# Output projection of all tokens in seven products of quarters, and a new order for the other seven products

## The chip, the cores and the metric

The kernel runs on one core of one Trainium2 chip, as one program in one launch. The metric is the device time of that program in microseconds (us); lower is better. The core has a matrix engine (TensorE, PE in the profile), three engines for elementwise work (VectorE or DVE, ScalarE or ACT, GpSimd or POOL) and a queue that issues the DMA transfers (SyncE or SP). Each engine runs its own instructions in order, and semaphores hold an instruction until what it needs is there. Matrix products go to PSUM, whose banks hold 128 x 512 fp32 values each; GpSimd reads and writes SBUF only in this kernel.

## The reference

All values are fp32. 1024 tokens (2 sequences of 512) of width 512 pass through four layers, each with a layer norm before it and a residual sum after it:

```python
x = x + block_sparse_linear(layernorm(x))
x = x + ffn(layernorm(x))        # gate and up: 512 -> 1792, dequantised; down: 1792 -> 512
x = x + mixer(layernorm(x))
x = x + ffn(layernorm(x))        # the same weights again

def mixer(h):                    # H=128 heads of P=64, INTER=8192, 8 groups, N=128, chunks of 128
    proj = h @ in_proj_w.T       # gate (8192), x (8192), B and C (8 x 128 each), dt (128)
    x, B, C = silu(causal_conv4(proj[x, B, C]))
    dt = softplus(dt + dt_bias);  A_dt = -exp(A_log) * dt
    y  = scan over chunks of (C B^T * decay) x_dt + C state + D * x
    y  = y * rsqrt(mean(y * y) + eps) * norm_w * silu(gate)
    return y @ out_proj_w.T      # 8192 -> 512
```

What the change touches are the matrix products of the mixer's input projection, of the gate and up projections of the feed-forward parts, and the mixer's output projection `y @ out_proj_w.T`.

## The kernel before

**Stages.** `block_sparse`, `ffn` (first), `mixer`, `ffn` (second). The normed input lies transposed in SBUF (`xn_t`: 4 chunks of 128 channels x 1024 tokens). The mixer works through its 8192 inner channels in 32 phases of 256 (two tiles of 128 channels, index j, by two sequences of 512 tokens, index b: four "units"). Phase `ph` runs three things side by side: the input projection of its own channels (x first, the gate later), the scan of the channels of the phase before (`c1`), and the output projection of the channels of the phase before that (`ph - 2`). Phases 2 to 30 are called `mid`; there are 29 of them. In seven of them (3, 7, ... 27) a new group of B and C channels is projected as well.

**Order.** Inside the kernel PE, ACT and DVE run in the order in which the program text issues their instructions (`manual_schedule`). The order of GpSimd and of the DMA queue is found by the framework's planner. So the places of `next(steps)`, `next(gate)`, `o()`, `drain(n)`, `flush()`, `back_scores(k)`, `all_squares()` in the phase loop are a schedule written by hand.

**Seven products of quarters.** A product of two matrices, each cut into 2 x 2 quarters, takes eight products of quarters; with sums of quarters made beforehand (Strassen's scheme in Winograd's form) seven do. `seven` (L177) does so for the projections: `left_sides` (L166, GpSimd) makes four sums of the weight's quarters, `tq` holds sums of the input's quarters, each of the seven products is two fp32 matmuls of 128 x 128 by 128 x 512 (each of which shows as two instructions in the profile), and the results are combined by accumulation in PSUM banks x, y, z, by one ScalarE copy (L202) and by five VectorE additions (L206, L211, L212, L220, L225). `seven` is a generator: each `next` issues one product with its sums, and the caller puts other work between. `done(j, b, result)` is called as a result is ready: for x, B and C that is `conv` (L730), one ScalarE pass and three VectorE taps that are kept back until `drain`; for the gate it notes a `silu` for later; in the feed-forward part it is the silu or the multiplication with it.

**Output projection.** In a `mid` phase the token blocks 0, 1, 4 and 5 (the first half of each sequence) go through `out_seven` (L1007): seven products of quarters, each two token blocks by 256 of the 512 columns, whose sums over phases are kept in `acc` (which is `x_sb`) and, for the product that three quarters share, in `common`. `o()` issues one of them with its VectorE sum (L1035). `out_left` (L998) makes four sums of the scan's outputs, `out_right` (L985) four of the weights, all on GpSimd. The blocks 2, 3, 6 and 7 go through `out_project` (L952) by `outs(k)`: two matmuls of 512 columns for each block and one VectorE addition (L969). The first phase and the last ones project all blocks by `out_project`; `merge` (L1055) adds `common` to the three quarters in phase 31.

**The other steps of a phase.** `tokens(k)` transposes one unit (PE, L828), multiplies it with dt (DVE, L832) and with the decay (GpSimd `x_dec`, L836). `back_scores(k)` and `half_scores(k)` make the decay matrix of one head (ACT, L893, L900, L903; GpSimd, L907); its product with the scores (DVE, L901) is kept back until `flush`. `both_states` multiplies `x_dec` with B (PE, L849) and carries states (DVE, L860, L863). `scan` (L915) issues the products of a unit into bank `py` (L920, L929); `skipped` (L940) reads that bank and `gated` (L943) gates the result; `all_squares` squares it (ACT, L949) and sums the squares (GpSimd, L950).

**PSUM.** Eight banks: three of tag `proj`, three of `yo` and two of `tr`. A bank is taken again when its last reader is done. The `yo` banks serve in one phase for the products of the output projection, for the two scans of `half_scan(units[:2])`, for the plain blocks and, in a phase without a new group, for two banks of the gate's seven. The weight tiles `w` of the input projection have two buffers; a DMA fills one (L606) as soon as the last product that reads its former content is done, and `left_sides` (L171 to L174) follows.

## Time and profile before

| What | Value |
|---|---|
| Runs | 2259.35, 2258.80, 2258.38 us; median 2258.8 |
| Span of the profiled execution, first to last instruction | 2256.4 us |
| TensorE granted clock, mean | 1.000 |
| HBM read and written | 194.91 MB and 4.72 MB |
| Busy in 400 to 1026 us (626.0) | PE 623.71, DVE 543.49, ACT 398.19, POOL 368.03 |
| Busy in 1182 to 1900 us (718.0) | PE 718.00, DVE 625.06, ACT 453.90, POOL 417.04 |
| Additions of `seven`, each | 0.68 to 0.69 us on DVE |
| Copy of `seven` (L202), each | 0.57 to 0.59 us on ACT |

The profile is of one execution. It gives its span; the runs' times hold also what lies before the first and behind the last instruction. "Busy" of TensorE comes from pipelined instructions: an instruction of 512 columns is shown as some 0.59 us long, though the next one starts 0.43 us after it. Durations are therefore best read from stretches of like instructions. In lists of groups the columns are line, engine and operation, output and inputs with their sizes and the number of instructions, then busy time in all, mean ns of one, and idle time before them with what ended it. In a timeline the columns are start, length, and the instruction or a run of like ones; in square brackets stands idle time before it and what ended it.

### The profile page before, as it was taken

Reading aid. Unit: us, or ns where it says so; the run is one execution under the profiler, and the core shown is the slowest. Engines: PE = TensorE matmul, PEld = TensorE weight load, DVE = VectorE, ACT = ScalarE, POOL = GpSimd, SP = SyncE. Lnnn points to the kernel's source line nnn. Section 1 sums busy time; section 2 is a strip of 40 time slices with the busy share of each in tenths; the row PEclk is TensorE's granted clock in tenths of the full one; section 3 lists DMA queues with packets and bytes.
Section 4 is the critical chain, followed back from the end, with each engine's and each line's share of the span. In section 5 each row is a group of like instructions: output and inputs, shape, how many; then the busy total and the mean of one; then the engine's idle time right before and its main releaser. Section 6 shows DMA issues by size and latency. Waiting matters only on the chain.

```text
span 2256.4 us, 29331 instructions
## 1 busy us (share of the span) xinstructions
PE 2241.1 (99%) x10356; PEld 1340.5 (59%) x10356; DVE 1766.8 (78%) x3017; ACT 1166.2 (52%) x2474; POOL 1193.9 (53%) x1202
## 2 busy tenths in 40 slices
PE   9999999999999999999999999999999999999999
PEld 5445875556665665665566656656655666544468
DVE  5456558888888888888888888888888989865552
ACT  4111056756665665666566656656665665731100
POOL 3765023655655566566556555665665564536610
PEclk9999999999999999999999999999999999999999
DMA  6563021222222222222222222221222322337500
GB/s 196 191 202 108 24 70 61 80 66 76 74 69 73 76 75 85 65 77 82 66 77 70 71 75 74 77 84 60 82 76 67 111 66 75 122 103 232 196 10 28
DMA packets 145779, 201.53 MB, mean 89 GB/s; under 512 B 7136, under 2 KB 92000, under 8 KB 145632
## 3 DMA queue, kind: packets, MB, share of 16 engines
q1 hardware_dynamic: 145056, 198.61, 27.7%
q8 instruction: 82, 1.34, 0.2%
q10 hardware_dynamic: 576, 1.05, 0.1%
q14 instruction: 65, 0.53, 0.1%
HBM read 194.91 MB, written 4.72 MB: 88 GB/s over the span
## 4 chain that ended last, share of the span: by engine, by line
PE 95%; DVE 3%; ACT 1%; issue 0%; POOL 0%; DVEq 0%; ACTq 0%; POOLq 0%
PE proj L185 31%; PE yo L185 19%; PE po L957 11%; PE po L1022 8%; PE ffn_o L557 7%; PE py L920 5%; PE pst L849 4%; PE py L929 4%; PE x_tr L828 2%; PE pg L487 1%; PE bs_o L336 1%; PE pu L487 1%; PE pgm L779 1%; DVE xc L735 1%; PE ln_tr L142 0%; PE stir L233 0%
## 5 line engine op out<-in xcount | busy, mean ns | idle before, releaser
L907 POOL TENSOR_TENSOR ce<-ce,c_t 128x384 f32<-128x384 f32 x256 | 288.5, 1131 | 318.3 <-ACT ce L903 312.6
L185 PE MATMUL proj<-xn_t,w 128*128 128x512 f32 x824 | 384.6, 593 | 2.0 <-DVE gt L206 1.7
L893 ACT ACTIVATE m<-bc,acs 128x128 f32<-128x128 f32 x1024 | 324.8, 389 | 6.8 <-PE py L920 5.8
L185 PEld LDWEIGHTS proj<-xn_t,w 128*128 128x128 f32 x824 | 153.0, 190 | 155.8 <-issue 146.3
L957 PE MATMUL po<-wo,gt 128*128 128x512 f32 x528 | 238.2, 599 | 0.4 <-DVE y L940 0.4
L171 POOL TENSOR_TENSOR ws<-w 128x256 f32<-128x256 f32 x96 | 74.0, 771 | 308.7 <-DMA w<-in_win_t_dram 269.9
L901 DVE TENSOR_TENSOR m<-m,gm 128x512 f32<-128x512 f32 x256 | 227.6, 907 | 11.3 <-ACT m L900 10.4
L735 DVE SCALAR_TENSOR_TENSOR xc<-proj,cw,xc 128x511 f32<-128x511 f32 (+2 forms) x288 | 214.6, 746 | 6.6
L950 POOL TENSOR_TENSOR sq_acc<-sq_acc,y 128x512 f32<-128x512 f32 x128 | 175.8, 1377 | 76.7 <-ACT y L949 76.5
L185 PE MATMUL proj<-tq,ws 128*128 128x512 f32 x432 | 199.2, 592 | 0.0
L920 PE MATMUL py<-m,x_dt 128*64 128x128 f32 x2048 | 181.4, 276 | 0.1
L900 ACT ACTIVATE m<-m 128x512 f32<-128x512 f32 x256 | 161.3, 630 | 7.4
L957 PEld LDWEIGHTS po<-wo,gt 128*128 128x128 f32 x528 | 96.3, 190 | 109.7 <-issue 103.9
L185 PE MATMUL yo<-tq,ws 128*128 128x512 f32 x336 | 153.4, 599 | 0.4 <-ACT acs L715 0.4
L185 PE MATMUL yo<-xn_t,w 128*128 128x512 f32 x328 | 151.0, 592 | 0.0
L929 PE MATMUL py<-ce,state 128*64 128x128 f32 x1536 | 149.7, 273 | 0.0
L920 PEld LDWEIGHTS py<-m,x_dt 128*64 128x64 f32 x2048 | 122.5, 137 | 30.0 <-issue 14.4
L949 ACT ACTIVATE y<-y 128x512 f32<-128x512 f32 x128 | 76.5, 623 | 110.3 <-DVE gt L943 110.3
L969 DVE TENSOR_TENSOR x_sb<-x_sb,po 128x512 f32<-128x512 f32 x136 | 92.9, 685 | 48.9 <-PE po L957 47.2
L903 ACT ACTIVATE ce<-bc 128x384 f32<-128x384 f32 x256 | 129.8, 507 | 0.0
L245 POOL TENSOR_TENSOR w<-w,sf 128x1024 f32<-128x1024 f32 (+1 forms) x30 | 70.0, 2335 | 112.9 <-DVE w L244 87.2
L732 ACT ACTIVATE xc<-proj,cb,cw 128x512 f32<-128x512 f32 x96 | 74.2, 775 | 105.8 <-DVE proj L225 76.6
(229 smaller groups left out, 4491.7 us busy)
## 6 DMA issues: line engine op xcount, KB each, us to landing
bc<-acs_d SPq DMA_DIRECT2D x128, 512.0 KB, 3.8
w<-in_win_t_dram SPq DMA_DIRECT2D x64, 512.0 KB, 3.8
wo<-in_wo_t_dram SPq DMA_DIRECT2D x31, 512.0 KB, 4.0
wi<-in_down_w_dram SPq DMA_DIRECT2D x14, 512.0 KB, 3.9
zi<-in_down_z_dram SPq DMA_DIRECT2D x14, 512.0 KB, 4.7
sf<-in_down_s_dram SPq DMA_DIRECT2D x14, 512.0 KB, 4.3
wi<-in_gate_w_dram SPq DMA_DIRECT2D x13, 512.0 KB, 4.2
zi<-in_gate_z_dram SPq DMA_DIRECT2D x13, 512.0 KB, 5.3
```

Source lines behind the costliest of these rows:

```text
L185: nc.tensor.matmul(ps, lhsT=a[:, kc, :], rhs=b[:, kc, :], start=(start and kc == 0), stop=(stop and kc == KH - 1), skip_group_check=True,)
L557: nc.tensor.matmul(ps, lhsT=a[:, k, :], rhs=b(k), start=(start and k == 0), stop=(stop and k == KF - 1), skip_group_check=True,)
L735: nc.vector.scalar_tensor_tensor(dst[:, s:], ps[:, : SEQ - s], cw[:, t, 3 - s : 4 - s], dst[:, s:], ALU.mult, ALU.add)
L893: nc.scalar.activation(m[:, c, :], bc[:, hh, c * P : (c + 1) * P], AF.Relu, bias=acs[:, t, h : h + 1], scale=-1.0,)
L900: nc.scalar.activation(m, m, AF.Exp, scale=-1.0)
L901: mults.append(lambda: nc.vector.tensor_mul(m, m, shared[b][2]))
L907: nc.gpsimd.tensor_mul(ce, ce, c_t[:, P:].rearrange("p (c l) -> p c l", l=P))
L920: nc.tensor.matmul(py[hh * HD : (hh + 1) * HD, c * P : (c + 1) * P], lhsT=x_dt[:, c, hh, :], rhs=m[:, c, :], start=True, stop=(c == 0),)
L929: nc.tensor.matmul(py[hh * HD : (hh + 1) * HD, c * P : (c + 1) * P], lhsT=state[:, c - 1, hh, :], rhs=ce[:, c - 1, :], start=False, stop=True,
L950: nc.gpsimd.tensor_add(sq_acc[:, b, :], sq_acc[:, b, :], y)
L957: nc.tensor.matmul(po, lhsT=gts[j, b][:, c * P : (c + 1) * P], rhs=wo[:, j, :], start=(j == 0), stop=(j == PP - 1),)
L1022: nc.tensor.matmul(banks[k][:, c, :], lhsT=a[:, t], rhs=b, start=(start and c == 0), stop=stop, skip_group_check=True,)
```

## The change

It has three parts.

1. *Output projection.* In the 29 middle phases all eight token blocks go through seven products of quarters: `out_seven` is called twice, for r = 0 (blocks 0, 1, 4, 5) and r = 1 (blocks 2, 3, 6, 7), and `o()` runs 14 times where it ran 7 times beside four `outs`. `out_left` makes its four sums for both halves, the second four at the start of the next phase. The tile `sums` grows from 4 to 7 rows, `common` to two tiles in one weight buffer, and `merge` adds both.
2. *Order of `seven`.* Products 1, 2 and 3 are now a11 b11, s1 t1 and s2 t2, each copied by ScalarE; s2 t2 accumulates on a11 b11, s4 b22 on s1 t1, s3 t3 and a22 t4 on the bank of the first. Three additions on VectorE remain, and the last result comes straight from PSUM. The third bank is opened at the sixth product. All users of `seven` are affected: x and gate of each phase, groups, feed-forward parts. The results come in the order (0,1), (1,1), (0,0), (1,0).
3. *Order of the phase.* `drain`, `flush`, `silu`, `all_squares`, `back_scores` and `half_scores` are put at other places between the products, in phases 0 to 31. The scores of a group are kept by sequence in a dictionary, since they can be made in either order.

The core of the diff (left out are the same kind of moves in phases 0, 1 and 31, the dictionary, and the place where `mid` is set):

```diff
@@ -196,34 +196,35 @@
         def bank(i):
             return psum.tile([P, SEQ], F32, tag=tags[i], name=f"{tags[i]}{i}", bufs=3)
 
-        x = bank(0)
-        c12, c21, c22 = tmp(0, 1), tmp(1, 0), tmp(1, 1)
-        product(x, a11, b11, True, False)
-        nc.scalar.copy(c21, x)
+        y = bank(0)
+        m1, m3, u2 = tmp(1, 0), tmp(1, 1), tmp(0, 1)
+        product(y, a11, b11, True, False)
+        nc.scalar.copy(m1, y)
         yield
-        y, z = bank(1), bank(2)
-        product(y, s2, t2, True, False)
-        nc.vector.tensor_add(c12, c21, y)
+        z = bank(1)
+        product(z, s1, t1, True, False)
+        nc.scalar.copy(m3, z)
         yield
-        product(z, s1, t1, True, False)
+        product(y, s2, t2, False, False)
+        nc.scalar.copy(u2, y)
+        yield
+        product(z, s4, b22, False, True)
+        r = z if in_place else u2
+        nc.vector.tensor_add(r, u2, z)
+        done(0, 1, r)
         yield
         product(y, s3, t3, False, False)
-        nc.vector.tensor_add(c22, c21, y)
-        nc.vector.tensor_add(c22, c22, z)
-        done(1, 1, c22)
+        nc.vector.tensor_add(m3, m3, y)
+        done(1, 1, m3)
         yield
-        product(x, a12, b21, False, True)
-        done(0, 0, x)
+        x = bank(2)
+        product(x, a12, b21, True, True)
+        r = x if in_place else m1
+        nc.vector.tensor_add(r, m1, x)
+        done(0, 0, r)
         yield
         product(y, a22, t4, False, True)
-        r = y if in_place else c21
-        nc.vector.tensor_add(r, c21, y)
-        done(1, 0, r)
-        yield
-        product(z, s4, b22, False, True)
-        r = z if in_place else c12
-        nc.vector.tensor_add(r, c12, z)
-        done(0, 1, r)
+        done(1, 0, y)
         yield
...
             quarter = [
-                (slice(b * NCH, b * NCH + 2), slice(n * DH, (n + 1) * DH)) for b in range(2) for n in range(2)
+                [
+                    (slice(b * NCH + 2 * r, b * NCH + 2 * r + 2), slice(n * DH, (n + 1) * DH))
+                    for b in range(2)
+                    for n in range(2)
+                ]
+                for r in range(2)
             ]
 
             def out_right(wo, s):
@@ -988,29 +994,32 @@
                 t = sides(True).rearrange("p i k c -> p i (k c)")
                 nc.gpsimd.tensor_sub(t[:, 0], b12, b11)
                 nc.gpsimd.tensor_sub(t[:, 1], b22, t[:, 0])
-                nc.gpsimd.tensor_sub(s[:, 3], b22, b12)
+                nc.gpsimd.tensor_sub(s[:, 6], b22, b12)
                 nc.gpsimd.tensor_sub(t[:, 2], b21, t[:, 1])
-                return b11, t[:, 0], b21, b22, t[:, 1], s[:, 3], t[:, 2]
+                return b11, t[:, 0], b21, b22, t[:, 1], s[:, 6], t[:, 2]
 
             def out_room():
-                return sc.tile([P, 4, DH], F32, tag="sums", name="sums")
-
-            def out_left(gts, s):
-
-                a11, a12, a21, a22 = [gts[j, b][:, : 2 * P] for b in range(2) for j in range(2)]
+                return sc.tile([P, 7, DH], F32, tag="sums", name="sums")
+
+            def out_left(gts, room, r):
+
+                toks = slice(2 * r * P, 2 * (r + 1) * P)
+                s = room[:, 3 * r : 3 * r + 3]
+                a11, a12, a21, a22 = [gts[j, b][:, toks] for b in range(2) for j in range(2)]
                 nc.gpsimd.tensor_add(s[:, 0], a21, a22)
                 nc.gpsimd.tensor_sub(a21, a11, a21)
                 nc.gpsimd.tensor_sub(s[:, 1], s[:, 0], a11)
                 nc.gpsimd.tensor_sub(s[:, 2], a12, s[:, 1])
                 return a11, a12, s[:, 0], s[:, 1], a21, s[:, 2], a22
 
-            def out_seven(left, right, fresh):
+            def out_seven(left, right, r, fresh):
 
                 a11, a12, s1, s2, s3, s4, a22 = left
                 b11, t1, b21, b22, t2, t3, t4 = right
-                if fresh:
-                    common.append(weights(True).rearrange("p kc j c -> p (kc j c)")[:, : 2 * DH].rearrange("p (t n) -> p t n", n=DH))
-                q11, q12, q21, q22 = [acc[:, rows, cols] for rows, cols in quarter]
+                if fresh and r == 0:
+                    both = weights(True).rearrange("p kc j c -> p (kc j c)").rearrange("p (r t n) -> p r t n", r=2, n=DH)
+                    common.extend([both[:, 0], both[:, 1]])
+                q11, q12, q21, q22 = [acc[:, rows, cols] for rows, cols in quarter[r]]
...
-                    ("x", True, False, a11, b11, common[0], True),
+                    ("x", True, False, a11, b11, common[r], True),
...
-                rows, cols = quarter[k]
-                nc.vector.tensor_add(acc[:, rows, cols], acc[:, rows, cols], common[0])
+                for r in range(2):
+                    rows, cols = quarter[r][k]
+                    nc.vector.tensor_add(acc[:, rows, cols], acc[:, rows, cols], common[r])
...
-                all_squares()
+                if not mid:
+                    all_squares()
...
                 if mid:
-                    outs7 = out_seven(lefts, rights, ph == 2)
+                    outs7 = out_seven(lefts, rights, 0, ph == 2)
+                    outs7 += out_seven(out_left(gts_old, room_o, 1), rights, 1, ph == 2)
 
                     def o():
                         product, summed = outs7.pop(0)
@@ -1225,23 +1236,31 @@
                         summed()
 
                     next(steps)
+                    all_squares()
                     tokens(2)
                     tokens(3)
                     flush()
                     o()
                     next(steps)
-                    back_scores(2)
+                    back_scores(1 if ph == 2 else 2)
                     o()
                     o()
-                    back_scores(3)
+                    if ph > 2:
+                        back_scores(3)
                     next(steps)
                     flush()
+                    if ph == 2:
+                        back_scores(2)
                     both_states(0)
                     o()
                     next(steps)
+                    if ph == 2:
+                        back_scores(3)
                     o()
                     next(steps)
                     drain(3)
+                    if ph == 2:
+                        flush()
                     o()
                     back_scores(4)
                     next(steps)
@@ -1253,46 +1272,56 @@
                     for skipped, _ in scans:
                         skipped()
                     gated = [f for _, f in scans]
-                    outs(2)
-                    flush()
+                    o()
+                    o()
                     back_scores(5)
-                    outs(3)
-                    gated[0]()
-                    flush()
+                    o()
+                    o()
                     back_scores(6)
                     if made:
                         group_scores(made, groups[c0 // CTG], [0])
-                    outs(6)
+                    o()
                     flush()
-                    back_scores(7)
+                    o()
+                    if not new_group:
+                        back_scores(7)
                     if made:
                         group_scores(made, groups[c0 // CTG], [1])
-                    outs(7)
+                    o()
                     flush()
-                    gated[1]()
-                    all_squares()
+                    for f in gated:
+                        f()
                     made = None
                     if new_group:
 
                         steps, made = group((c0 + PP) // CTG, wbc, "yo")
                         for i, _ in enumerate(steps):
-                            if i in (1, 3, 5):
+                            if i == 1:
+                                all_squares()
+                            if i in (1, 2, 5):
                                 drain(3)
+                            if i == 2:
+                                back_scores(7)
+                            if i == 5:
+                                flush()
                         gate, later = g_front(wg, gts_new)
                     else:
                         gate, later = g_front(wg, gts_new, ("proj", "yo", "yo"))
                         next(gate)
+                        next(gate)
+                        all_squares()
                     wx = load_pair(NCT + c0 + PP, NCT + c0 + PP + 1)
...
-                        lefts, rights = out_left(gts, room_o), out_right(wo, room_o)
+                        lefts, rights = out_left(gts, room_o, 0), out_right(wo, room_o)
                     if new_group:
                         next(gate)
+                        next(gate)
                     half_scores(0, c0, heads_new)
+                    drain(3)
                     next(gate)
-                    drain(3)
                     half_scores(1, c0, heads_new)
                     next(gate)
                     next(gate)
@@ -1300,19 +1329,18 @@
                     for u in units:
                         silu(xcs_new[u], xcs_new[u])
                     flush()
-                    next(gate)
                     if not new_group:
                         drain(3)
                     run(gate)
```

## The prediction

> **What bounds the kernel now.** I read the page first: the busy shares, the granted clock and the chain of work that ended last. They say that TensorE is the bound over nearly the whole span, at full clock, and that VectorE is next.
>
> ```profile
> PE 2241.1 (99%) x10356; PEld 1340.5 (59%) x10356; DVE 1766.8 (78%) x3017; ACT 1166.2 (52%) x2474; POOL 1193.9 (53%) x1202
> PEclk9999999999999999999999999999999999999999
> PE 95%; DVE 3%; ACT 1%; issue 0%; POOL 0%; DVEq 0%; ACTq 0%; POOLq 0%
> ```
>
> Next, the list of waits for TensorE alone. Its largest entries are 3.0, 1.9 and 1.7 us, one wait or two each, and the whole list is some 12 us. So the kernel becomes faster by issuing fewer matmul columns, and every new wait of TensorE is paid in full.
>
> Then one ordinary phase of the 29 in the middle of the mixer (1026.03 to 1074.21, between two like places) in the view by stages, and its pieces in the chain:
>
> ```profile
> 1026.03:1074.21 48.18, 48.18 (x253) 29.39 (x253) 42.13 (x74) 30.94 (x69) 29.84 (x33) 1.00 0.24 77
> 1030.34 1.72 PE proj L185 x4
> 1033.39 0.87 PE po L1022 x4
> 1048.26 7.06 PE po L957 x16
> ```
>
> The first line holds stretch, length and busy time of PE, its weight load, DVE, ACT and POOL: TensorE 48.18 of 48.18, VectorE 42.1, ScalarE 30.9, GpSimd 29.8. Four instructions (two fp32 products) of 512 columns take 1.72 us, 0.429 each; four of 256 take 0.863, 0.2157 each. Half the width costs half, so nothing is lost by narrow products. The 16 wide ones of the plain output projection take 7.06, where 16 x 0.429 is 6.86; the 0.2 more stands at the edges to the narrow scan products.
>
> **Step 1, the columns.** Each middle phase drops out_project for blocks 2, 3, 6 and 7: four blocks, two products, two instructions, so 16 of 512 columns: 6.86 us. It adds seven products of two blocks with 256 columns, 28 instructions: 28 x 0.2157 = 6.04. Net -0.82 a phase, 29 x -0.82 = -23.8 us. If the edge of 0.2 went too it would be -1.02, or -29.6; the narrow products stand between the same neighbours, so I take -23.8.
>
> **Step 2, VectorE's and ScalarE's work.** The phase has two sevens of quarters of the input projection. Each loses two VectorE additions of 0.69 and gains two ScalarE copies of 0.57. The output projection exchanges four additions of 0.69 for seven. VectorE: -4 x 0.69 + 3 x 0.69 = -0.7 a phase. ScalarE: +2.3. GpSimd: four more sums of 0.73, +2.9. New totals 41.4, 33.2 and 32.7 of some 47.4: none becomes a bound by its sum. What counts is which wait ends last.
>
> **Step 3, the wait that I expect.** Times below count from the first transposition of a phase. In the old phase:
>
> ```profile
> 1022.40 1.04 PE L828 MATMUL x_tr<-ident,xc 128*128 128x128 f32 x8
> 1026.73 1.88 PE L185 MATMUL proj<-tq,ws 128*128 128x512 f32 x4
> 1048.19 7.13 PE L957 MATMUL po<-wo,gt 128*128 128x512 f32 x16
> 1026.24 1.28 ACT L893 ACTIVATE m<-bc,acs 128x128 f32<-128x128 f32 x4
> 1031.08 0.63 ACT L900 ACTIVATE m<-m 128x512 f32<-128x512 f32 x1
> 1028.72 0.69 DVE L206 TENSOR_TENSOR tmp<-tmp,proj 128x512 f32<-128x512 f32 x1 [1.10 <-PE proj L185]
> 1030.98 2.79 DVE L901 TENSOR_TENSOR m<-m,gm 128x512 f32<-128x512 f32 x2
> 1033.70 0.28 DVE L860 COPY state<-pst 128x128 f32<-128x128 f32 x1
> 1047.79 1.40 DVE L940 SCALAR_TENSOR_TENSOR y<-xc,dsk,py 128x512 f32<-128x512 f32 x2
> ```
>
> ScalarE (L893) began the scores of head 2 at 3.84, with only the copy of the first product ahead. Now a copy of the second product (m3) is queued in front. That product ends at 1028.61, and its reader began at 1028.72, so at 6.3; the copy moves the queue on by 0.46 (1025.78 to 1026.24), so the scores begin at 6.8, 2.9 later. Queued behind that copy are both heads' scores, the copy u2 and VectorE's multiplications. The second exponential ended 5.47 after the start of the scores (1026.24 to 1031.71): now 12.25. VectorE's second multiplication then takes 0.61 (the pitch of two without GpSimd: 1.28 for two at 1021.00) to 1.36 (half of the 2.79 and a little), and the states begin at 12.9 to 13.7, where they began at 11.3.
>
> From there to the end of the first skip addition took 1033.70 to 1048.49, 14.8; the new order has one addition fewer in it (-0.6) and drops a wait of 0.29 for ScalarE: 13.9. So the first bank of the scan comes free at 26.8 to 27.6. Who needs it? The three banks of tag yo hold po7 sums and the two scan outputs; the second of the new seven products opens a bank, and its only candidates are the two scan banks. TensorE reaches it at 25.79 (where the plain block stood) + 0.86 + 0.11 of edge = 26.8. The old block needed that bank one wide product later, at 27.6, against 26.1 when it was free. So the wait is 0.05 to 0.85 a phase. In a phase where the multiplication had waited for its exponential as it will now, it took 1.05 (1141.82), which gives about 0.45; a wait in one place also gives slack to the later ones, so I take 0.4: 29 x 0.4 = +11.6.
>
> The Trainium skill, page "SBUF — State Buffer", section "Who interferes with whom", speaks against the change: a VectorE instruction with two SBUF inputs contends with a GpSimd instruction that reads SBUF. The slow 1.36 while GpSimd works is in line with it. By the rule the four added GpSimd sums would push the multiplication to its slow price, 0.85 a phase and a time near 2261; by the row of 1.05 it is the 0.4 above.
>
> **Step 4, waits costed at nothing, with their cover.** Product 5 of the seven must wait for the copy u2: behind both heads' scores it ends at 13.1, product 5 begins at 14.3: cover 1.2. In the gate's seven the same copy stands behind two squares and one head's scores; my count puts it at 41.5 to 42.2 against 42.4, cover 0.2 to 0.9. Product 7 must wait for the addition of m3 on VectorE: 18 against 19.4. If one of these covers is gone, TensorE stops in place, and VectorE catches up, so the next cover grows.
>
> The w buffer's last reader moves from the sixth product to the seventh, so SP's load of the next weights is issued 1.72 later. GpSimd waits for this load in order:
>
> ```profile
> 1024.96 0.73 POOL L171 TENSOR_TENSOR ws<-w 128x256 f32<-128x256 f32 x1 [5.06 <-DMA w<-in_win_t_dram]
> 1027.83 0.84 POOL L836 TENSOR_TENSOR x_dec<-x_dt,dec 128x384 f32<-128x384 f32 x1
> 1031.89 1.50 PE L849 MATMUL pst<-x_dec,b_tok 128*128 128x128 f32 x12
> ```
>
> L171 came 4.1 after the end of the sixth product (1020.85); now at 4.3 instead of 2.6, and the second x_dec ends 3.7 later, at 8.0, against the state products at 9.5. Cover 1.5, so nothing, if the four new sums run in the 5 us for which GpSimd idles before L171.
>
> **Step 5, the rest.** Three more merges in the final phase at 1.24 (L1058: 3.6 for three): between 0 and 3.7, I take +1.0, since TensorE's sevens stand back to back there. The sevens of the feed-forward parts, the groups and phase 0: the copies take 0.57 and have a product of 1.72 between, so 0; bounds are -5.6 (all waits of TensorE for VectorE and ScalarE in these parts go) and +7 (0.25 in some 28 sevens). Longer sums and commons are storage only.
>
> **Sum:** -23.8 + 11.6 + 1.0 = -11.2; span 2256.4 - 11.2 = 2245.2. The median of the runs shown, 2258.8, is 2.4 above the profiled span, which is the work around it: **2247 us**.
>
> **The rivals.**
> - *Forecast, 45%:* 0.05 to 0.65 a phase at the scan bank, 2237 to 2255.
> - *No wait holds TensorE, 17%:* for it, the covers of step 4 and the fact that the columns alone set the phase now; against it, the scan bank. -23.8 and 1.0 give 2236; with the edge gone, 2231.
> - *VectorE's order eats it all, 20%:* 0.85 a phase against 0.82 gained gives 2258.8 + 0.9 + 1.0 = 2261. For it, the 1.36 multiplication and the tight gate; against it, VectorE's 41.4 of 47.4.
> - *Slower, 18%:* the four new GpSimd sums are put between L171 and the second x_dec. Then x_dec ends at 8.0 + 2.9 = 10.9, the state products wait 1.4 a phase, the scan bank is no wait any more, and the phase is 1.4 - 0.82 = 0.58 longer: +17, with the merges 2277. For it: GpSimd's order isn't written by hand, and the new sums stand in the program right behind x_dec's tokens. Against it: their inputs are ready before, and GpSimd interleaves its sums now (L1001 to L1004 among L907). It decides from a lateness of 0.82 a phase on.
>
> **How the numbers follow.** The likeliest case is the forecast, 2247, with its own range 2237 to 2255. For 8 in 10 I go down to 2232, in the case without waits, and up to 2268, half way into the slower case. 0.2% is 4.5 us, about what a measurement of this kernel can tell from no change: faster means under 2254.3, slower over 2263.3. Faster: the case without waits and nearly all of the forecast, 0.62; same: the rest of it and most of the third, 0.20; slower 0.18.
>
> **What would show it.** Right: 28 po instructions of 256 columns at 0.216 in each middle phase, none of 512; a phase of about 47.8 in place of 48.18; one wait of TensorE of a few tenths for the skip addition (y, L940 as it is numbered now) at the second narrow product behind the scans. No wait there: the case without waits. A wait of the state products for GpSimd's x_dec: the slower case. Waits of products 5 or 7 of a seven for ScalarE's copies or VectorE's m3 would show that step 4's covers are wrong, and a phase over 48.2 that the whole forecast is.

## The result, and the profile after

The changed kernel takes 2295.78 us (median of four runs, 2293.99 to 2296.26), against 2258.95 for the kernel before on the same chip: a ratio of 1.0162, with a 95% interval of 1.0148 to 1.0177. It is slower by 37 us, where 2247 (2232 to 2268) was forecast. The profiled span went from 2256.4 to 2294.4 us, at a granted clock of 1.00 in both. Lines of the program have moved by one or more: the skip addition is now L941, the transposition L829, the narrow products L1031.

From the page of the changed kernel, the busy shares and the shares of the chain that ended last:

```profile
span 2294.4 us, 30367 instructions
PE 2247.2 (98%) x10704; PEld 1400.4 (61%) x10704; DVE 1700.4 (74%) x2915; ACT 1280.6 (56%) x2666; POOL 1281.9 (56%) x1318
PE 59%; DVE 20%; ACT 10%; POOL 4%; DMA 4%; issue 2%; SPq 0%; POOLq 0%; DVEq 0%
```

The busy share of TensorE fell by one point only, from 99% to 98%. The chain shows much more: TensorE held 95% of it and holds 59% now. For two fifths of the span something else decides when the kernel ends, though VectorE, ScalarE and GpSimd are each busy for less than three quarters of the time. So what went wrong is the order of work, not the amount of it. One ordinary phase in the view by stages (length; then busy time and count of PE, weight load, DVE, ACT, POOL):

```profile
1039.21:1088.81 49.60, 48.43 (x265) 31.33 (x265) 40.19 (x73) 33.36 (x73) 32.55 (x37) 1.00 0.22 75
```

It was 48.18 long, all of it TensorE's. Phases come in fours: one that projects a new group, one right behind it (the group is "made" there), and two ordinary ones. From first transposition to first transposition the lengths of a typical four are, in us:

| kernel | with group | behind it | ordinary | ordinary | mean |
|---|---|---|---|---|---|
| before | 60.20 | 50.63 | 48.18 | 48.18 | 51.80 |
| after | 61.92 | 51.78 | 48.94 | 49.60 | 53.06 |

The phases 3 to 30 together became 36.9 us longer, of the span's 38.0; that is 1.32 each, a little more than in the typical four, since some phases were longer. The stages ahead of phase 1 became 1.1 longer, phase 1 3.7 shorter, phase 2 2.4 longer and the last phase 1.1 longer; from phase 32 on, the second feed-forward part included, it is 307.4 in both. So nearly all of the loss is in the middle phases. What TensorE waits for there, in the list of its waits within 340 to 1950 us (total, times, longest):

```profile
PE po L1031 <- DVE y L941: 18.9, 29, 1.7
PE x_tr L829 <- ACT gt L751: 10.1, 15, 0.7
PE proj L185 <- DVE gt L217: 3.3, 11, 1.0
```

These are 32.3 us of idle time. The timeline of TensorE in an ordinary phase shows where they lie, and that the time lost is more than this idle time (start, length, instructions; in brackets the idle time and its releaser):

```profile
1062.59 1.13 PE L1031 MATMUL po<-wo,gt 128*128 128x256 f32 x4
1064.07 1.99 PE L1031 MATMUL po<-ws,sums 128*128 128x256 f32 x8 [0.34 <-DVE y L941]
...
1081.52 1.88 PE L185 MATMUL yo<-xn_t,w 128*128 128x512 f32 x4
1083.55 1.98 PE L185 MATMUL proj<-tq,w 128*128 128x512 f32 x4
...
1086.25 1.88 PE L185 MATMUL proj<-xn_t,w 128*128 128x512 f32 x4
1088.81 1.22 PE L829 MATMUL x_tr<-ident,xc 128*128 128x128 f32 x8 [0.68 <-ACT gt L751]
```

Four narrow instructions have a pitch of 0.86 and four wide ones of 1.72. So the second narrow product should have begun at 1063.45 and is 0.62 late; the gate's last product is 1083.55 - 81.52 - 1.72 = 0.31 late; the second run of transpositions (units 2 and 3) is 1088.81 - 86.25 - 1.72 = 0.84 late, and 0.19 more is lost inside it. Over the four kinds of phase, the scan bank costs 0.61, 0.62 and 0.63, and 1.70 where the group is made (mean 0.89); the transposition 0.29 to 1.03, what is lost inside it included (mean 0.68); the gate's last product 0.31 in two of four (0.16); a scan in the group phase 0.60 (0.15). These are 1.88 a phase. With about 0.2 of smaller delays and -0.82 of columns that makes 1.26, which is the table's 53.06 - 51.80.

The transposition is the wait that the prediction doesn't have at all. The chain of waits leads back from it:

```profile
1068.72 4.61 DMA wo<-in_wo_t_dram
...
1073.46 0.87 POOL ws L995
...
1075.80 1.28 POOL ws L998
1077.07 1.24 POOL sq_acc L951
...
1078.34 0.76 DVE y L941
1079.12 0.96 DVE gt L944
...
1085.72 1.74 DVE m L902 x2
1087.46 0.61 DVE gt L223
1088.10 0.64 ACT gt L751
...
1088.81 1.22 PE x_tr L829 x8
```

Read from the bottom: the transposition comes when VectorE reaches the end of its list for the phase. VectorE is late because the skip addition of the last unit (L941) waits for a room: the tile `y` has three, and the sum of squares on GpSimd (L951) has to free one. GpSimd does that sum late because the planner put the sums of the next output weights (L995 to L998) ahead of it, and these stand still for 4.6 us until the load of `wo` lands.

The load itself isn't late. It is issued when the last product that reads the old `wo` is done, 29.5 us after the second run of transpositions (1039.21 to 1068.72). In the kernel before the plain blocks read `wo` as late, and it was issued 30.4 us after them (1024.99 to 1055.39). What has moved are the squares. In the kernel before, ScalarE squared the first two `y` at 1053.31 and 1057.66, and GpSimd summed them ahead of the sums of the weights. From its timelines of the DMA queue and of GpSimd:

```profile
1055.39 0.37 SPq L793 DMA_DIRECT2D wo<-in_wo_t_dram  x1
...
1054.70 1.72 POOL L950 TENSOR_TENSOR sq_acc<-sq_acc,y 128x512 f32<-128x512 f32 x1
1058.37 1.28 POOL L950 TENSOR_TENSOR sq_acc<-sq_acc,y 128x512 f32<-128x512 f32 x1 [1.96 <-ACT y L949]
1059.61 0.72 POOL L989 TENSOR_TENSOR ws<-wo 128x256 f32<-128x256 f32 x1
```

In the changed kernel the gating of these two `y` stands behind the last narrow product and `all_squares` behind the gate's second product. ScalarE squares them from 1073.65 on, when the load has landed, and GpSimd takes the weights first. In the whole run GpSimd stood idle for this load ahead of the first of these sums 26 times, 119.0 us in all, and in the kernel before 3 times, 2.4 us.

The chain names ScalarE's silu (L751) as the last link. The transposition doesn't read it; in the program it needs a bank of tag `tr`, which the multiplication with dt (L833) frees, and that stands on VectorE right behind L223:

```profile
1087.99 1.27 DVE L833 TENSOR_TENSOR x_dt<-x_tr,dt 128x512 f32<-128x512 f32 x2
```

The first of the two ends at about the same instant as the silu (1088.7), so this trace alone can't tell which of them releases (e1 below can). Both stand behind L223.

### The profile page after: what moved, and what is told of

Same layout as the page of the kernel before. It is cut to its first block, busy times and chain, and to the rows that moved or that the text cites. A ratio compares the mean times of both kernels' runs of the same rounds, so it can differ in the third digit from the quotient of the medians.

```text
span 2294.4 us, 30367 instructions
## 1 busy us (share of the span) xinstructions
PE 2247.2 (98%) x10704; PEld 1400.4 (61%) x10704; DVE 1700.4 (74%) x2915; ACT 1280.6 (56%) x2666; POOL 1281.9 (56%) x1318
## 4 chain that ended last, share of the span: by engine, by line
PE 59%; DVE 20%; ACT 10%; POOL 4%; DMA 4%; issue 2%; SPq 0%; POOLq 0%; DVEq 0%
PE proj L185 19%; PE yo L185 12%; PE ffn_o L558 7%; PE po L1031 7%; DVE xc L736 6%; ACT m L894 4%; DMA wo<-in_wo_t_dram 3%; DVE state L864 2%; DVE m L902 2%; PE py L921 2%; DVE x_sb L1044 2%; PE po L958 2%; PE x_tr L829 2%; PE pst L850 1%; PE py L930 1%
## 5 line engine op out<-in xcount | busy, mean ns | idle before, releaser
L908 POOL TENSOR_TENSOR ce<-ce,c_t 128x384 f32<-128x384 f32 x256 | 277.5, 1091 | 259.7 <-ACT ce L904 254.9
L1044 DVE TENSOR_TENSOR x_sb<-x_sb,po 128x512 f32<-128x512 f32 x340 | 230.4, 683 | 61.3 <-PE po L1031 61.3
L902 DVE TENSOR_TENSOR m<-m,gm 128x512 f32<-128x512 f32 x256 | 199.8, 810 | 88.5 <-ACT m L901 88.5
L185 PE MATMUL proj<-tq,ws 128*128 128x512 f32 x520 | 242.9, 597 | 0.0
L951 POOL TENSOR_TENSOR sq_acc<-sq_acc,y 128x512 f32<-128x512 f32 x128 | 167.8, 1324 | 17.1 <-ACT y L950 17.0
L171 POOL TENSOR_TENSOR ws<-w 128x256 f32<-128x256 f32 x96 | 74.5, 776 | 180.5 <-DMA w<-in_win_t_dram 165.6
L837 POOL TENSOR_TENSOR x_dec<-x_dt,dec 128x384 f32<-128x384 f32 x128 | 122.3, 969 | 68.6 <-DVE x_dt L833 31.4
L185 PEld LDWEIGHTS proj<-tq,ws 128*128 128x128 f32 x520 | 96.7, 190 | 91.0 <-issue 87.1
L185 PE MATMUL proj<-tq,w 128*128 128x512 f32 x304 | 144.6, 598 | 4.6 <-DVE gt L217 3.3
L1031 PE MATMUL po<-ws,sums 128*128 128x256 f32 x464 | 114.3, 390 | 20.4 <-DVE y L941 18.9
L941 DVE SCALAR_TENSOR_TENSOR y<-xc,dsk,py 128x512 f32<-128x512 f32 x128 | 92.7, 744 | 50.8 <-POOL sq_acc L951 27.1
```

The source lines that it names most:

```text
L185: nc.tensor.matmul(ps, lhsT=a[:, kc, :], rhs=b[:, kc, :], start=(start and kc == 0), stop=(stop and kc == KH - 1), skip_group_check=True,)
L902: mults.append(lambda: nc.vector.tensor_mul(m, m, shared[b][2]))
L908: nc.gpsimd.tensor_mul(ce, ce, c_t[:, P:].rearrange("p (c l) -> p c l", l=P))
L951: nc.gpsimd.tensor_add(sq_acc[:, b, :], sq_acc[:, b, :], y)
L1031: nc.tensor.matmul(banks[k][:, c, :], lhsT=a[:, t], rhs=b, start=(start and c == 0), stop=stop, skip_group_check=True,)
L1044: nc.vector.tensor_add(q, q, banks[k])
```

## The experiments

Each is timed against the kernel before on the same chip; the ratios are to it. Each kernel is the changed one with the edit shown, unless another is named.

### Which half of the change costs the time

**e1: the new order alone.** The plain projection of blocks 2, 3, 6 and 7 is put back.

```diff
-                    outs7 += out_seven(out_left(gts_old, room_o, 1), rights, 1, ph == 2)
...
-                    o()
-                    o()
+                    outs(2)
                     back_scores(5)
-                    o()
-                    o()
+                    outs(3)
                     back_scores(6)
```

> The changed kernel with its output projection put back: seven products for blocks 0, 1, 4, 5 and four plain blocks for the rest; the new order of the other seven products and of the phase stays. My theory: the loss comes from waits that the new order makes (VectorE late at the end of a phase, behind a y tile that GpSimd's squares hold, behind the load of wo), not from the narrow products. Then 29 x some 1.0 us stays: about 2288 us (2278 to 2296), with waits of the transposition of units 2 and 3. Rival, the narrow products of the output projection are what costs: 2250 to 2262 us.

Measured: 2290.64 us, 1.0140 (1.0125 to 1.0155), within its range. Nearly all of the loss is there without one additional narrow product. Phases are 61.4, 51.5, 48.9 and 49.1; the gate's last product and the transposition are late here too, and the plain block waits for the scan bank in the phase where the group is made (0.83).

This run also tells what releases the transposition. Here the third silu of the gate, which the chain of the changed kernel names, ends at 1033.15, after the transposition has begun; the first multiplication with dt ends at 1032.79, 0.15 ahead of it:

```profile
1032.94 1.23 PE L829 MATMUL x_tr<-ident,xc 128*128 128x128 f32 x8
1031.49 1.66 ACT L751 ACTIVATE gt<-gt 128x512 f32<-128x512 f32 x3
1032.11 1.28 DVE L833 TENSOR_TENSOR x_dt<-x_tr,dt 128x512 f32<-128x512 f32 x2
```

The same 0.15 stands between them wherever the transposition is late, in the changed kernel, e3, e4 and e8 too. So it is the bank, and VectorE, that it waits for.

**e2: the output projection alone.** The kernel before, with 14 narrow products and its own seven and order.

```diff
-                    outs(2)
+                    o()
+                    o()
                     flush()
                     back_scores(5)
-                    outs(3)
+                    o()
+                    o()
                     gated[0]()
```

> The kernel before with only its output projection changed: all eight blocks in 14 narrow products, at the places of the four plain blocks; the old order of the other seven products and of the phase. My theory: the columns are worth 0.82 us a phase and the scan's bank is free in time in the old order (26.1 against 26.8): 2235 us, up to 2246 if some waits stay. Rival, the narrow products are what costs: 2275 us or more.

Measured: 2269.48 us, 1.0049 (1.0034 to 1.0064), between the two expectations. The phase with a made group has no new wait, and it went from 50.63 to 49.81: the -0.82 of the columns, exactly. The others wait in a place that neither theory named. From the waits of TensorE and the timeline of VectorE of e2:

```profile
PE po L1030 <- DVE x_sb L1043: 21.7, 22, 1.0
```

```profile
1056.23 0.75 DVE L943 SCALAR_TENSOR_TENSOR gt<-y,nw,gt 128x512 f32<-128x512 f32 x1
1056.89 0.69 DVE L901 TENSOR_TENSOR m<-m,gm 128x512 f32<-128x512 f32 x1
1057.49 1.28 DVE L1043 TENSOR_TENSOR x_sb<-x_sb,po 128x512 f32<-128x512 f32 x2
```

Narrow products follow each other every 0.86 us and each wants an addition of 0.6 to 0.7. A gating and a multiplication between two additions put VectorE 1.3 behind, and the last product waits 1.16 for its bank. A plain block gave VectorE one addition for 1.72 us of TensorE (four instructions of 0.43), so there was room for them.

### The waits of the new order, one by one

**e3: the scores of head 2 ahead of the copy of m3**, which is the cause that the prediction named for the scan bank.

```diff
                     o()
-                    next(steps)
                     back_scores(1 if ph == 2 else 2)
+                    next(steps)
                     o()
```

> The changed kernel with the scores of head 2 issued ahead of the second product of x, so that ScalarE doesn't hold them behind the copy of that product. My theory of the wait at the second narrow product behind the scans (0.6 us a phase, 1.7 where a group was made): it goes, 29 x 0.6 to 0.9 less: 2270 to 2279 us. Rival, that wait is set by something else or moves on: 2290 to 2296 us.

Measured: 2286.77 us, 1.0128 (1.0111 to 1.0145), 9 below the changed kernel where 16 to 26 were expected. The wait at the scan bank is gone in ordinary phases and those with a group, but is 1.79 still where the group is made, and part of the gain is handed on: the gate's last product is now 0.63 to 0.88 late instead of 0.31. The cause is right, its worth was estimated as if the next wait weren't there.

**e4: the sums of the weights behind the sums of squares** on GpSimd.

```diff
-                        lefts, rights = out_left(gts, room_o, 0), out_right(wo, room_o)
+                        lefts = out_left(gts, room_o, 0)
+                        with tc.issue_after(squared[-1].ins):
+                            rights = out_right(wo, room_o)
```

> The changed kernel with GpSimd's four sums of the output weights queued behind the sums of squares, so that the squares don't stand behind the load of wo. My theory of the wait at the transposition of units 2 and 3 (1.0 us in half of the phases) and at the gate's last product (0.3): VectorE gets its y tile 1.9 us sooner and both go, some 0.9 a phase: 2268 to 2276 us. Rival, VectorE is late there because of its own order: 2288 to 2296 us.

Measured: 2288.44 us, 1.0133 (1.0118 to 1.0148). The skip addition doesn't wait for the squares any more, and the gate's last product isn't late, but the transposition still is (0.84 became 0.5, and in the mean over the phases, with what is lost inside, 0.68 became 0.58), and the scan bank waits 0.77. So the link through GpSimd is real, and by itself it explains less than half of the transposition's delay. The rival's price was right.

**e6: the multiplications of the next heads kept back** to the next phase, which takes two of 0.9 us out of the end of VectorE's list.

```diff
                         silu(xcs_new[u], xcs_new[u])
-                    flush()
                     if not new_group:
```

> The changed kernel with VectorE's two multiplications of the next heads kept back from the end of a middle phase to the flush behind the transpositions of units 2 and 3. Theory now: the transposition of units 2 and 3 waits for a tr bank that VectorE's x_dt frees, and x_dt stands behind VectorE's tail of the phase (taps, two multiplications of some 0.9, an addition). 1.8 us less in that tail: that wait goes (0.3 to 1.0 a phase), the one at the scan's bank and the gate's last product stay: 2270 to 2280 us. Rival, it is the silu of the gate on ScalarE that the profile names as the releaser: no change, 2293 to 2297 us.

Measured: 2271.80 us, 1.0058 (1.0043 to 1.0073), as expected: 24 us for one line. The transposition waits no longer, and the phases are 61.0, 50.5, 48.6 and 48.5. In the timeline of VectorE the addition and the multiplication with dt now follow the taps directly:

```profile
1074.51 0.68 DVE L223 TENSOR_TENSOR gt<-gt,yo 128x512 f32<-128x512 f32 x1
1075.10 1.28 DVE L833 TENSOR_TENSOR x_dt<-x_tr,dt 128x512 f32<-128x512 f32 x2
```

So VectorE's tail holds the transposition. Not all of the 24 us are this wait: the wait at the scan bank where the group is made fell as well, from 1.70 to 0.67, which the expectation had left standing; why wasn't followed.

**e8: one product of the gate ahead of the second scans instead of two.**

```diff
                         next(gate)
-                        next(gate)
                         all_squares()
...
                     if new_group:
                         next(gate)
-                        next(gate)
+                    next(gate)
                     half_scores(0, c0, heads_new)
```

> The changed kernel with one gate product ahead of the second scan, as before, and not two. Theory: the second gate product ahead of the scan takes 1.72 us of TensorE's work from behind it, which covered VectorE's tail from that scan to x_dt. With it back, the waits at the transposition and at the gate's last product go, some 0.9 a phase: 2266 to 2276 us. Rival, VectorE is held by the y tile and the load of wo, which don't move: 2288 to 2298 us.

Measured: 2306.53 us, 1.0214 (1.0199 to 1.0230). Neither expectation covers it. The theory that putting the product back would end these waits fell. The second scans now come earlier, VectorE waits longer for GpSimd's squares (2.65 where it was 1.85), and the transposition 1.1:

```profile
1082.12 0.75 DVE L941 SCALAR_TENSOR_TENSOR y<-xc,dsk,py 128x512 f32<-128x512 f32 x1 [2.65 <-POOL sq_acc L951]
```

What comes earlier on TensorE brings nothing while the skip addition waits for a load and for the planner's order. What the moved product costs once that order is mended wasn't run.

### The mends together

**e7: e3, e4 and e6 in one kernel.**

```diff
-                    next(steps)
                     back_scores(1 if ph == 2 else 2)
+                    next(steps)
...
+                        with tc.issue_after(squared[-1].ins):
+                            rights = out_right(wo, room_o)
...
-                    flush()
```

> The changed kernel with three edits at once: scores of head 2 ahead of the second product, squares ahead of the sums of output weights on GpSimd, the two multiplications kept back. If the waits are what costs and don't come back elsewhere: 2235.1 for the columns alone, and what is left at the scan's bank in phases behind a new group (7 x 1.7) and at the second scan of the seven group phases (7 x 0.6): some 2251 us (2245 to 2258). Rival, each wait removed shows up at the next place: over 2270 us.

Measured: 2249.04 us, 0.9958 (0.9941 to 0.9974), faster than the kernel before. The phases are 60.3, 50.5, 47.55 and 47.55: an ordinary phase is 0.63 below the old 48.18, the 0.82 of the columns less 0.19. The 0.19 is lost at the last narrow product, which accumulates in the bank that VectorE's sum of the fifth one reads. It begins as this sum ends, 0.08 late, and loses 0.10 more inside. In e12, further down, whose ordinary phases are as long, the sum ends at 1043.65:

```profile
1042.96 0.69 DVE L1045 TENSOR_TENSOR x_sb<-x_sb,po 128x512 f32<-128x512 f32 x1 [0.17 <-PE po L1032]
...
1043.70 1.13 PE L1032 MATMUL po<-ws,gt 128*128 128x256 f32 x4
```

It is the link that costs e2 1.16. Where a group is made, its scores stand between these products, and nothing is lost.

**e13: e7 without e4's edit**, to see whether that one is needed behind the others.

```diff
-                        with tc.issue_after(squared[-1].ins):
-                            rights = out_right(wo, room_o)
+                        rights = out_right(wo, room_o)
```

> As e7_three_mends, without the edit of the squares on GpSimd: scores of head 2 first, multiplications kept back. Theory: the y tile that the squares hold behind the load of wo still makes VectorE late by some 1.9 us, which without the multiplications costs no more than 0.2 to 0.5 a phase at the gate's last product: 2255 to 2264 us. Rival, it costs nothing then: 2249 us as e7.

Measured: 2261.47 us, 1.0013 (1.0004 to 1.0023). GpSimd's order is worth 12 us here and was worth 7 alone, where both ratios are uncertain by some 3 us. The time lies at the gate's last product, which is late by 0.59 again, as the waits of TensorE in e13 show:

```profile
PE proj L185 <- DVE gt L217: 8.7, 13, 2.0
```

**e10: two more mends on e7**: the squares go behind the scores of head 3, for the phase in which the group is made; and in the group phase head 7's scores go to their usual place and the `flush` at the group's sixth product falls away.

```diff
                     next(steps)
-                    all_squares()
                     tokens(2)
...
                         back_scores(3)
+                    all_squares()
...
-                    if not new_group:
-                        back_scores(7)
+                    back_scores(7)
```

> As e7_three_mends, and the squares of the phase before go behind the scores of head 3 on ScalarE, and head 7's scores of a group phase stand where they stand in the others. Theory of the 1.7 in a phase behind a new group: ScalarE's scores start late there, behind silu, two squares (1.05) and two copies. Less 7 x 0.7 to 1.0 and 7 x 0.6 than e7: 2241 us (2236 to 2250). Rival: no less than e7.

Measured: 2243.98 us, 0.9935 (0.9921 to 0.9950). The phase behind a new group went from 50.5 to 49.82, which is again 50.63 - 0.82. The second mend brought nothing by itself: the group phase went from 60.3 to 60.5, since a product of the group now waits 0.6 for a bank that a narrow product's sum frees.

**e12: e10 with two places of `flush` mended**, one in the group phase and one in the last phase.

```diff
                     o()
-                    flush()
+                    if not new_group:
+                        flush()
                     o()
...
+                    if ph == n_ph - 2:
+                        flush()
```

> As e10_five_mends, with two small moves: in a group phase the multiplications of heads 4 to 6 wait until the fifth and sixth sums of the second seven are done (in e10 the group's second product waited 0.6 there for a bank that such a sum frees), and in the last middle phase the two multiplications aren't kept back (the phase behind it went from 50.9 to 51.4). Theory: 7 x 0.6 and 0.6 less than e10: 2239 us (2236 to 2242). Rival, the group's wait moves on: 2243 to 2245.

Measured: 2239.94 us, 0.9918 (0.9903 to 0.9933). It beats both kernels: 56 us less than the changed one, 18.7 less than the one before. The phases are 59.94, 49.82, 47.55 and 47.56. Its page and its ordinary phase:

```profile
PE 2223.7 (99%) x10704; PEld 1400.9 (63%) x10704; DVE 1738.3 (78%) x2915; ACT 1280.2 (57%) x2666; POOL 1279.2 (57%) x1318
PE 97%; DVE 1%; ACT 1%; POOL 0%; DMA 0%; issue 0%; SPq 0%; DVEq 0%; POOLq 0%
```

```profile
1012.54:1060.09 47.55, 47.55 (x265) 31.51 (x264) 42.89 (x73) 33.42 (x73) 32.63 (x37) 1.00 0.25 78
```

The counts of instructions on each engine are those of the changed kernel; only the order differs. TensorE fills 47.55 of 47.55 and has 97% of the chain.

### Could the old seven have done it?

**e14: e2 with the changed kernel's order of work behind the first scans.**

```diff
                     o()
-                    gated[0]()
-                    flush()
                     back_scores(6)
...
-                    gated[1]()
+                    for f in gated:
+                        f()
                     all_squares()
```

> The kernel before with its output projection changed as in e2_output_only, and VectorE's work behind the first scans in the order of the changed kernel (multiplications and gating behind the fifth sum, not between the first ones). In e2 the last narrow product waited 1.2 us a phase for a sum that stood behind them. Theory: the columns alone make the kernel faster, and the new order of the other seven products isn't needed for it: the wait goes, 2236 us (2233 to 2244). Rival, the old order of seven leaves VectorE no room for three more sums: 2255 us or more.

Measured: 2327.24 us, 1.0303 (1.0287 to 1.0318), 91 above what was expected. The theory that e2 lacks only this order fell. In the waits of TensorE in e14:

```profile
PE yo L185 <- DVE gt L206: 49.5, 21, 3.6
```

The old seven has a VectorE addition behind its second product; with the gatings and squares at the end of VectorE's list, the gate's fourth product waits 2.9 for it. The new seven has a ScalarE copy in that place.

**e15: e2 with the first gating and two multiplications moved by three narrow products.**

```diff
                     o()
-                    gated[0]()
-                    flush()
                     back_scores(6)
...
                     o()
+                    gated[0]()
                     flush()
```

> As e2_output_only, with one gating and two multiplications put behind the sixth sum of the second seven, and the rest of VectorE's order left as it was (e14 had put both gatings behind the last sum, and the gate's fourth product then waited 2.9 us a phase for the first VectorE addition of its seven). Theory: the only wait of e2, 1.2 us at the last narrow product, goes, and the addition comes no later than in e2: 2239 us (2235 to 2247), so the old order of the other seven products will do. Rival, the addition comes later and the gate's fourth product waits: 2255 us or more.

Measured: 2257.82 us, 0.9997 (0.9988 to 1.0006): no change from before. The ordinary phases became 0.2 to 0.3 shorter and the one where the group is made 0.4, but the group phase 0.4 longer and the last one 2.1, and small delays for the old seven's additions remain. Whether a better order exists for the old seven stays open.

## Why the prediction was wrong

**Step 1, the columns: right.** -0.82 a phase is what the phase without a wait shows: 49.81 (e2) and 49.82 (e10, e12) against 50.63. In the other phases 0.19 is lost to VectorE's sum at the last narrow product (e7), so it is -0.63 in an ordinary one; the prediction doesn't have this wait.

**Step 2, the totals: right.** 41.4, 33.2 and 32.7 were forecast for VectorE, ScalarE and GpSimd; 40.2, 33.4 and 32.6 came out. No engine became a bound by its sum, and the kernel is slower all the same.

**Step 3, the scan bank: the mechanism right, the term too small.** The place (the second narrow product behind the scans), the reader (the skip addition) and the cause (the copy of m3 ahead of the scores, e3) are those forecast. The second multiplication began at 13.3 from the phase's first transposition, and I had 12.25 with 12.9 to 13.7 for the states; the 1.0 between them is the lateness of the transposition in that phase, which TensorE has as well. The term was 0.4 a phase and 0.89 was measured. In ordinary phases it is 0.62; the rest is the phase where the group is made, at 1.70, where ScalarE has more ahead of the scores. I worked out one ordinary phase and multiplied by 29. The slow price of the multiplication wasn't needed: the second one took 0.69 with GpSimd's `x_dec` beside it (1049.09, 1.32 long, where the one before took 0.96).

**Step 4 is the step that failed.** "Waits costed at nothing, with their cover" listed the copies and the m3 additions, and most of these covers held; only the gate's last product lost 0.31 in two phases of four. What it lacks is the wait of the transposition, 0.68 a phase in the mean. I followed each step that moved to its next reader, and didn't follow the end of VectorE's list to the first thing that TensorE needs in the next phase. Two causes are shown there. The multiplications of the next heads stand at the end of VectorE's list (e6); they stood there before too, but the first bank came free 0.8 earlier than it was needed (the first multiplication with dt began at 1071.58 and takes 0.68, so it ended at 1072.26; the transposition began at 1073.17, and 0.15 lies between the two where it waits). And the skip additions need a room that GpSimd frees (e4): the diff moves the squares behind the gate's second product, and the planner then put the sums of the weights, with their load, ahead of them. The load of `wo` is no later than before. In step 4 I followed the load of `w` past one product, and didn't follow the moved squares to the room that they free and on to the skip addition behind it. That one product of the gate, 1.72, now runs ahead of the second scans also takes cover from VectorE's tail; e8 doesn't show what that alone costs.

**Step 5: right.** The last phase became 1.1 longer, where 1.0 was taken for its merges, and the second feed-forward part is unchanged. The stages ahead of phase 1 (1.1 longer) and phases 1 and 2 (-1.3 together) weren't counted.

**The sum.** 2245.2 and 2.4 are 2247.6, not 2247; and the work around the span is 1.7 in the runs (2296.10 against 2294.4), so 2246.9 would have been the figure. This changes nothing in the outcome.

**The rivals.** The slower case had the right sign and the right engine: GpSimd's order, which the planner makes. It had the wrong place. The second `x_dec` isn't behind the new sums: both `x_dec` stand ahead of L171 now, and the new sums run before the phase begins, as the timeline of GpSimd shows:

```profile
1039.14 1.63 POOL L837 TENSOR_TENSOR x_dec<-x_dt,dec 128x384 f32<-128x384 f32 x2 [0.41 <-DVE x_dt L833]
1040.72 0.73 POOL L171 TENSOR_TENSOR ws<-w 128x256 f32<-128x256 f32 x1
```

Its 18% was too little, and 2277 too low. "VectorE's order eats it all" bounded the loss at 0.85 a phase through the scan bank; the waits cost 1.9. "No wait holds TensorE" gave 2236, or 2231 with the edge gone; e12 reached 2239.94 when the order was mended, so the sum for that case was right within 4 us and its condition wasn't met.

**What the mends add up to.** Alone, e3, e4 and e6 gave 9.0, 7.3 and 24.0 us, 40.3 in all; together 46.7. The difference is about what the intervals allow, but e3 and e13 show directly that time freed at one wait was partly taken by the next one, the gate's last product.

## What to carry to other kernels

Where one engine is full, a saving of its arithmetic is worth only what the order of the other engines lets through: here 24 us of columns were outweighed by 53 us of waits on engines that are busy for 56 to 74% of the span. When work is moved or cut up, follow the end of each engine's list into the next round, to the first instruction of the full engine that needs it, with the rooms of tiles and the PSUM banks that a last reader releases among the links; and work out each kind of round, not the ordinary one alone. Where one engine's order comes from a planner and the others' from hand, look at which of its instructions stand behind a load.

## What the hardware showed unexpectedly

The list of waits shows less than the waits cost. Idle time is counted from the shown end of the instruction before, and in a stream the next one starts 0.16 ahead of that end (0.59 shown and 0.43 apart; 0.38 and 0.22 for 256 columns). So 0.68 idle is 0.84 late, and the gate's last product, 0.31 late, isn't in brackets at all. A block that has waited is also longer itself: four narrow instructions 1.13 where 1.03 is usual, four wide ones 1.98 for 1.88, eight transpositions 1.22 for 1.04. So the 32.3 us of listed waits stand for some 53 (1.88 for 28 phases).

On VectorE the three taps of a unit take 2.31 us where the first operand lies in PSUM, and in both kernels one result of the seven is in SBUF instead. In the kernel before, its taps took 2.32 us; in the changed kernel 2.95:

```profile
1038.76 2.32 DVE L735 SCALAR_TENSOR_TENSOR xc<-tmp,cw,xc 128x511 f32<-128x511 f32 x3 [0.29 <-ACT xc L732]
1041.70 1.00 POOL L907 TENSOR_TENSOR ce<-ce,c_t 128x384 f32<-128x384 f32 x1 [5.49 <-ACT ce L903]
...
1057.63 2.95 DVE L736 SCALAR_TENSOR_TENSOR xc<-tmp,cw,xc 128x511 f32<-128x511 f32 x3
1057.46 1.00 POOL L908 TENSOR_TENSOR ce<-ce,c_t 128x384 f32<-128x384 f32 x1 [6.09 <-ACT ce L904]
...
1083.41 2.31 DVE L736 SCALAR_TENSOR_TENSOR xc<-proj,cw,xc 128x511 f32<-128x511 f32 x3
1083.65 0.72 POOL L1010 TENSOR_TENSOR gt<-gt 128x256 f32<-128x256 f32 x1
```

The first two lines are of the kernel before, where GpSimd is idle during the taps; in the next two it multiplies beside them, and in the last two it works beside taps whose first operand is in PSUM, which take no longer. So neither the place of the operand nor GpSimd's work costs anything alone; both together cost some 0.6 us. In the kernel before, GpSimd is idle during all 32 such sets of taps, and each takes 2.31 to 2.32; in the changed kernel it is idle during one of the 32, which takes 2.32, and the others take 2.80 us or more.
